# Interpolating attention biases along x on TensorE in every other block of keys, in the first image's heads

## The chip, the cores and the metric

The kernel runs on one core of a Trainium2 chip, as one launch. Its time is the device time of that core in microseconds; a kernel is run several times and the median is quoted. A core has five engines, each with its own queue of instructions that it works through in order: TensorE (PE in the profile; PEld is its loading of weights), VectorE (DVE), ScalarE (ACT), GpSimd (POOL) and SyncE (SP), which here only issues DMAs. Engines wait for each other through semaphores. Matmul results land in PSUM, which VectorE and ScalarE read; all other tiles lie in SBUF.

## The reference

The program takes four images of 32 x 32 positions with 384 channels through four layers. The change lies in the first layer, an attention with sampled keys (shortened):

```
q   = x @ w_q + b_q                                  # per image: 1024 positions, 6 heads of 64
pos = ref + tanh(offset network of q) * 16           # one sampling position per key and group
xs  = bilinear_sample(x, pos)
k, v = xs @ w_k + b_k, xs @ w_v + b_v
attn = einsum('bhmc,bnhc->bhmn', q, k) * 64**-0.5
disp = (ref of query m - pos of key n) * 0.5
bias = bilinear_sample(rpe table of the head, disp)  # one number per head, query and key
attn = softmax(attn + bias)
out  = einsum('bhmn,bnhc->bmhc', attn, v) @ w_out + b_out
```

For one key, all 1024 queries read the table at the same fractions in x and y, shifted by whole steps. So the biases of a key are a window of the table, interpolated along y with two weights and along x with two weights, all four belonging to that key alone. The layers behind it (a second attention, a normalisation by window sums and an attention over 3 x 3 neighbours) are not touched.

## The kernel before, in words

Images follow each other in two lanes. `Front` does the first layer, `Trunk` the other three. The first layer of image 0 stands alone at the start; those of images 1 to 3 are interleaved with the trunk. For image 0 the heads are done by `Front.heads0`, for the others by `Front.head0`, which the change leaves as it is. While `heads0` runs, only the first steps of image 1's front (`early0`: transposes, group norm) are put between its turns.

`heads0` walks over 96 blocks: 6 heads, 2 halves of the queries (512 each), 8 blocks of 128 keys. Keys lie on the 128 partitions, queries along the free axis, so a block is a tile of 128 x 512. `turn(t)` is one step of a software pipeline and issues work for several blocks, at fixed distances from t. Nearly every instruction is wrapped in `pin`, which keeps program order on its engine; the few that are not may be moved by the framework's scheduler. Tiles come from rings by tag, and a tile's first writer waits until the buffer's last reader is done.

Of block b, in the order in which its work comes:

- turn b - 10: POOL gathers the window of the bias table by an indirect DMA (`win`, L918, 6 buffers).
- turn b - 6: ACT starts the interpolation along y (`z`, L949, 4 buffers): the window's rows times one weight, 16 x 33 numbers a key.
- turn b - 5: DVE adds the rows below times the other weight (L930). ACT starts the interpolation along x (`lg`, L940, 20 buffers): columns 0 to 31 times one weight.
- turn b - 4: DVE adds columns 1 to 32 times the other weight (L935). `lg` now holds the biases.
- even turns: TensorE makes the products of keys and queries for blocks t + 2 and t + 3 (L960), into the two halves, two PSUM banks, of one of two `big` tiles. One 128 x 512 product of 32-bit numbers is two matmul instructions in the trace.
- turn b: DVE adds the product to `lg` (L980) and takes the running maximum over the blocks of the half (L985).
- at the end of a half's 8 blocks: TensorE transposes the maximum (L990), DVE reduces it (L971), POOL makes a diagonal (L975), TensorE multiplies it with ones (L1015) and ACT copies the result (`tb`, L994).
- turn b + 10: DVE subtracts `tb` (L999), ACT takes the exponential (L1000).
- turn b + 11: TensorE multiplies with the values and with ones (L1009), 64 columns of the array each.
- one turn after a half's last such product: ACT copies the result over the queries in `qpad` (L1024) and the denominator row into a dead `lg` tile (L1029), from which SP sends it to memory. Later `divide` brings the reciprocals back into two `lg` tiles and DVE multiplies.

Inside a turn the order on DVE is z, lg, (reduction,) add, maximum, subtraction; on ACT it is lg, the next block's z, (`tb`,) exponential; on POOL the gather, then the diagonal; on TensorE the products of the pair, (transposes,) the value products.

Of the kernel before, what the change touches and what calls it, by code (L numbers as in the profile page):

```python
# [21 lines left out]
ALU = mybir.AluOpType  # L22
# [393 lines left out]
class Front(Lane):  # L416
# [447 lines left out]
    def heads0(self, work):  # L864

        nc, v, pin = self.nc, self.nc.vector, self.tc.keep_in_program_order
        f, va = self.f, self.va
        HH, HN = HW // 2, N // 2  # L870
# [2 lines left out]
        n = len(blocks)  # L873

        AHEAD, SUB, OUT = 5, 10, 11
        win, z, lg, ps, half, dens, inv = {}, {}, {}, {}, {}, {}, {}

        def tile_of(shape, tag, bufs):
            return work.tile(shape, F32, tag=tag, name=self.nm(tag), bufs=bufs)
# [8 lines left out]
        def divide(step, k):  # L888
            heads = (2 * k, 2 * k + 1)
            by_row = lambda a: a.rearrange("o (p i) -> (o p) i", p=P)  # L890
            if step == 0:
                dens[k] = tile_of([P, 2, NJ], "dens", 2)
                for r, h in enumerate(heads):
                    nc.sync.dma_start(dens[k][:, r, :], by_row(self.den[h]))
            elif step == 1:
                pin(v.reciprocal(dens[k], dens[k]))
                for r, h in enumerate(heads):
                    nc.sync.dma_start(by_row(self.rden[h]), dens[k][:, r, :])
                for q in range(2):
                    inv[q] = tile_of([P, HN], "lg", 20)  # L900
                    for r, h in enumerate(heads):
                        nc.sync.dma_start(
                            inv[q][r * GC : (r + 1) * GC],
                            self.rden[h][0, q * HN : (q + 1) * HN].partition_broadcast(GC),
                        )
            else:
                for q in range(2):
                    out = queries(2 * k, q)
                    w = inv[q].rearrange("p (y x) -> p y x", x=HW)
                    pin(v.tensor_tensor(out, out, w, ALU.mult))  # L910

        def turn(t):
            i = t + AHEAD

            if i + 5 < n:
                h, q, j = blocks[i + 5]
                win[i + 5] = tile_of([P, (HH + 1) * WROW], "win", 6)
                nc.gpsimd.indirect_dma_start(  # L918
                    out=win[i + 5],
                    out_offset=None,  # L920
                    in_=self.strips[:, :],
                    in_offset=bass.IndirectOffsetOnAxis(
                        ap=self.widx[:, q, j * G + h : j * G + h + 1], axis=0
                    ),
                )
            at = lambda i: blocks[i][2] * G + blocks[i][0]
            sc = lambda i, axis, side: f[:, side, axis, at(i) : at(i) + 1]
            if 0 <= i < n:
                wv = win.pop(i).rearrange("p (r c) -> p r c", c=WROW)
                pin(v.scalar_tensor_tensor(  # L930
                    z[i], wv[:, 1 : HH + 1, 0 : HW + 1], sc(i, 1, 0), z[i], ALU.mult, ALU.add
                ))
            if 0 <= i - 1 < n:
                zi, lf = z.pop(i - 1), lg[i - 1].rearrange("p (y x) -> p y x", x=HW)
                pin(v.scalar_tensor_tensor(  # L935
                    lf, zi[:, :, 1 : HW + 1], sc(i - 1, 0, 0), lf, ALU.mult, ALU.add
                ))
            if 0 <= i < n:
                lg[i] = tile_of([P, HN], "lg", 20)
                pin(nc.scalar.activation(  # L940
                    lg[i].rearrange("p (y x) -> p y x", x=HW),
                    z[i][:, :, 0:HW],
                    AF.Copy,
                    scale=sc(i, 0, 1),
                ))
            if 0 <= i + 1 < n:
                wv = win[i + 1].rearrange("p (r c) -> p r c", c=WROW)
                z[i + 1] = tile_of([P, HH, HW + 1], "z", 4)
                pin(nc.scalar.activation(  # L949
                    z[i + 1], wv[:, 0:HH, 0 : HW + 1], AF.Copy, scale=sc(i + 1, 1, 1)  # L950
                ))

            if t >= -2 and (t + 2) % 16 == 0 and t + 18 < n and t + 2 >= 16:
                self.load_keys(blocks[t + 18][0])
            if t >= -2 and t % 2 == 0 and t + 2 < n:
                big = self.big()
                for u in range(2):
                    h, q, j = blocks[t + 2 + u]
                    ps[t + 2 + u] = big[:, u * 512 : (u + 1) * 512]
                    pin(nc.tensor.matmul(  # L960
                        ps[t + 2 + u],
                        self.kz[h % 2][:, j * P : (j + 1) * P],
                        queries(h, q),
                        start=True,
                        stop=True,
                    ))

            m = (t - 1) // NJ
            if t > 0 and t % NJ == 0 and t <= n:
                top = tile_of([P, NI], "top", 2)  # L970
                pin(v.tensor_reduce(  # L971
                    top, half[m, "t"].rearrange("p (i n) -> p i n", i=NI), AX.X, ALU.max
                ))
                diag = tile_of([P, NI, P], "diag", 1)
                pin(nc.gpsimd.tensor_tensor(  # L975
                    diag, bc(self.ident, 1, NI), bc(top, 2, P), ALU.mult
                ))
            if 0 <= t < n:
                m, j = divmod(t, NJ)
                pin(v.tensor_tensor(lg[t], ps.pop(t), lg[t], ALU.add))  # L980
                if j == 0:
                    half[m] = tile_of([P, HN], "rmax", 2)
                else:
                    first = lg[t - 1] if j == 1 else half[m]
                    pin(v.tensor_tensor(half[m], first, lg[t], ALU.max))  # L985
                if j == NJ - 1:
                    half[m, "t"] = self.bank()
                    for i in range(NI):
                        cols = slice(i * P, (i + 1) * P)
                        pin(nc.tensor.transpose(half[m, "t"][:, cols], half[m][:, cols], self.ident))  # L990
            if t > 1 and t % NJ == 1 and t <= n + 1:
                m = (t - 2) // NJ
                half[m, "b"] = tile_of([P, HN], "tb", 2)
                pin(nc.scalar.copy(half[m, "b"], half[m, "p"]))  # L994

            s = t - SUB
            if 0 <= s < n:
                tb = half[s // NJ, "b"]
                pin(v.tensor_tensor(lg[s], lg[s], tb, ALU.subtract))  # L999
                pin(nc.scalar.activation(lg[s], lg[s], AF.Exp))  # L1000

            o = t - OUT
            if 0 <= o < n:
                h, q, j = blocks[o]
                if j == 0:
                    half[o // NJ, "o"] = self.bank()
                po = half[o // NJ, "o"]
                for own, w in ((True, va[:, j, h * GC : (h + 1) * GC]), (False, self.ones[:, 0:GC])):
                    pin(nc.tensor.matmul(  # L1009
                        po[rows(h, own), :], w, lg[o], start=j == 0, stop=j == NJ - 1  # L1010
                    ))
            if t > 0 and t % NJ == 0 and t <= n:
                m = (t - 1) // NJ
                half[m, "p"] = self.bank()
                pin(nc.tensor.matmul(  # L1015
                    half[m, "p"], self.ones, diag.rearrange("p i n -> p (i n)"),
                    start=True, stop=True,
                ))

            o = t - OUT - 1  # L1020
            if 0 <= o < n and o % NJ == NJ - 1:
                h, q, j = blocks[o]
                po, own = half[o // NJ, "o"], rows(h, True)
                pin(nc.scalar.copy(  # L1024
                    queries(h, q)[own], po[own, :].rearrange("p (y x) -> p y x", y=HH)
                ))
                o0 = rows(h, False).start
                den = lg[o][o0 : o0 + 1, :]
                pin(nc.scalar.copy(den, po[o0 : o0 + 1, :]))  # L1029
                nc.sync.dma_start(self.den[h][:, q * HN : (q + 1) * HN], den)  # L1030

            o = t - OUT - 2
            for step, late in enumerate((0, 4, 9)):
                if o >= late and (o - late) % (4 * NJ) == 4 * NJ - 1:
                    divide(step, (o - late) // (4 * NJ))
# [831 lines left out]
```

## Time and profile before

| what | value |
|---|---|
| median of 3 runs | 4702.68 us (4702.3 to 4724.38) |
| the profiled execution: its own time | 4728.0 us |
| the profiled execution: span | 4726.2 us |
| busy over the span | PE 88%, DVE 68%, ACT 49%, POOL 20% |
| first product of keys and queries in `heads0` (L960) | 217.8 us |
| last product of keys and queries | 541.5 us |
| last value products (L1009) | 560.3 us |
| mean granted clock of TensorE, whole span | 0.927 |

Times inside the kernel are microseconds from the start of the profiled execution's span. In a line of the time line the columns are start, length, engine, source line, operation, tiles written and read, and in brackets the idle time before it with what ended that. In a table by stretch each engine has its busy time and, in brackets, its instructions; then come the granted TensorE clock as a share of full speed, the DMA engines' share and GB/s. A group's line gives the count, then busy time in us and mean length in ns, then idle time before. A shown length includes the filling and draining of the engine's pipeline, so the next instruction may start before the last has ended: the distance from start to start is the time that an instruction takes from its engine. A TensorE that is busy may still run at a lower clock.

### The profile page before, as it was taken

The page shows a single profiled execution, that of the slowest core. Times are in us where ns is not written, and L with a number is a line of the kernel's source. Part 1 is how long each engine was busy: PE and PEld are TensorE (multiplying, and loading weights), DVE is VectorE, ACT ScalarE, POOL GpSimd, SP SyncE. Part 2 cuts the span into 40 slices and gives each one's busy share as a digit, 9 for nine tenths or more (in the row PEclk, how much of TensorE's full clock was granted, in tenths as well). Part 3 has the DMA queues.
Part 4 walks back from the last instruction along what each step waited for, and adds up shares of the span by engine and source line. Part 5 has one row for each costly group of instructions (what it writes and reads, how often), then busy time and mean ns, then how long its engine had stood idle before and what let it go on. Part 6 is the DMA issues. An engine that isn't in the chain of part 4 may idle for free. (4 is left out here: it accounts for less than half of the span.)

```text
span 4726.2 us, 46786 instructions
## 1 busy us (share of the span) xinstructions
PE 4162.4 (88%) x15704; PEld 1784.0 (38%) x15704; DVE 3212.5 (68%) x6013; ACT 2295.6 (49%) x3631; POOL 944.9 (20%) x946
## 2 busy tenths in 40 slices
PE   5477788999999988899999989799999998999998
PEld 2222233333333353333333444243333335344444
DVE  3599756777878727587878763767787884565654
ACT  2166423566656313466666432346565651455532
POOL 0533204221212103321211110421121211000000
PEclk8688888999999988999999989899999998999998
DMA  6435224321212143321211124521121213311011
GB/s 122 132 112 151 66 93 127 95 64 54 70 37 68 54 142 117 116 69 51 79 53 55 58 78 116 157 85 55 37 79 51 74 37 110 110 27 30 19 40 40
DMA packets 231730, 369.98 MB, mean 78 GB/s; under 512 B 117508, under 2 KB 164705, under 8 KB 231489
## 3 DMA queue, kind: packets, MB, share of 16 engines
q1 hardware_dynamic: 170472, 200.51, 14.5%
q0 software_dynamic: 39936, 145.53, 10.5%
q10 hardware_dynamic: 21080, 20.96, 1.8%
q8 instruction: 124, 2.03, 0.2%
q14 instruction: 118, 0.96, 0.1%
HBM read 287.41 MB, written 79.78 MB: 78 GB/s over the span
## 5 line engine op out<-in xcount | busy, mean ns | idle before, releaser
L1479 PE MATMUL bank<-whole,sg 128*128 128x512 f32 (+3 forms) x2304 | 862.1, 509 | 8.7 <-POOL sg L1432 6.9
L1488 DVE SCALAR_TENSOR_TENSOR e<-bank,gam,e 128x512 f32<-128x512 f32 x768 | 562.2, 749 | 445.3 <-ACT gn L1487 159.0
L1331 ACT ACTIVATE big<-big,nmax 128x1024 f32<-128x1024 f32 x384 | 418.7, 1090 | 405.9 <-DVE nmax L1330 368.8
L1457 ACT ACTIVATE e<-big 128x1024 f32<-128x1024 f32 x384 | 379.8, 1019 | 410.1 <-PE big L1449 404.4
L1479 PEld LDWEIGHTS bank<-whole,sg 128*128 128x128 f32 x2304 | 407.2, 199 | 375.3 <-issue 284.4
L1330 DVE TENSOR_REDUCE nmax<-big 128x1 f32<-128x1024 f32 x384 | 454.8, 1219 | 75.1 <-PE big L1322 33.0
L797 POOL DMA_INDIRECT win<-strips,widx x288 | 307.7, 1069 | 686.9 <-DVE z L810 415.2
L1432 POOL TENSOR_SCALAR sg<-whole,gam 128x512 f32<-128x512 f32 x192 | 152.0, 794 | 1454.4 <-PE bank L1479 1005.2
L1449 PE MATMUL big<-qa,ka 64*128 64x512 f32 x1536 | 423.3, 623 | 8.8 <-ACT big L1331 8.6
L1322 PE MATMUL big<-k,q 32*128 32x512 f32 x1536 | 325.3, 681 | 68.1 <-ACT e L1457 41.8
L818 PE MATMUL bank<-qpad,kz 128*128 128x512 f32 x576 | 283.9, 622 | 12.5 <-DVE e L1488 12.5
L712 POOL DMA_INDIRECT gat<-pairs,sidx x192 | 204.3, 1064 | 436.7 <-DVE sidx L526 241.5
L853 PE MATMUL bank<-lg,va 128*64 128x512 f32 x576 | 264.9, 604 | 15.0 <-ACT lg L851 14.9
L853 PE MATMUL bank<-lg,ones 128*64 128x512 f32 x576 | 264.3, 603 | 0.0
L815 DVE SCALAR_TENSOR_TENSOR lg<-z,bias_f,lg 128x512 f32<-128x512 f32 x288 | 220.7, 775 | 41.0 <-ACT lg L814 38.7
L809 ACT ACTIVATE z<-win,bias_f 128x528 f32<-128x528 f32 x288 | 208.8, 739 | 68.6 <-DVE lg L815 29.7
L1449 PEld LDWEIGHTS big<-qa,ka 64*128 64x128 f32 x1536 | 137.7, 186 | 264.2 <-issue 153.4
L810 DVE SCALAR_TENSOR_TENSOR z<-win,bias_f,z 128x528 f32<-128x528 f32 x288 | 214.6, 763 | 26.8 <-ACT z L809 19.4
L850 DVE TENSOR_TENSOR lg<-lg,tb 128x512 f32<-128x512 f32 x288 | 187.4, 697 | 42.4 <-ACT tb L843 42.4
L1421 PE MATMUL bank<-e,vs 128*32 128x512 f32 x1536 | 206.7, 604 | 0.9 <-DVE vs L1415 0.9
L819 DVE TENSOR_TENSOR lg<-bank,lg 128x512 f32<-128x512 f32 x288 | 192.5, 685 | 21.7 <-PE bank L818 20.5
L814 ACT ACTIVATE lg<-z,bias_f 128x512 f32<-128x512 f32 x288 | 200.6, 720 | 13.6 <-PE bank L853 7.0
(302 smaller groups left out, 6646.2 us busy)
## 6 DMA issues: line engine op xcount, KB each, us to landing
pairs<-xn SPq DMA_DIRECT2D x64, 192.0 KB
q<-qd SPq DMA_DIRECT2D x48, 256.0 KB
w<-in_gmat SPq DMA_DIRECT2D x16, 576.0 KB
w<-in_w_off SPq DMA_DIRECT2D x12, 576.0 KB
w<-in_Wqkv SPq DMA_DIRECT2D x12, 576.0 KB
a<-in_x SPq DMA_DIRECT2D x16, 384.0 KB
x<-a ACTq DMA_DIRECT2D x4, 1536.0 KB
win<-strips,widx POOLq DMA_INDIRECT x384
```

Source lines behind the costliest of these rows:

```text
L797: nc.gpsimd.indirect_dma_start(out=win, out_offset=None, in_=self.strips[:, :], in_offset=bass.IndirectOffsetOnAxis(ap=self.widx[:, q, c : ...
L810: v.scalar_tensor_tensor(z, wv[:, 1 : HH + 1, 0 : HW + 1], sc(0, 1), z, ALU.mult, ALU.add)
L815: v.scalar_tensor_tensor(lg, z[:, :, 1 : HW + 1], sc(0, 0), lg, ALU.mult, ALU.add)
L818: nc.tensor.matmul(ps, kz[:, j * P : (j + 1) * P], both, start=True, stop=True)
L853: nc.tensor.matmul(po[out, :], w, lf, start=j == 0, stop=j == NJ - 1)
L1322: nc.tensor.matmul(ps[r][:, h * 512 : (h + 1) * 512], self.q4[rows, i * P : (i + 1) * P], self.k4[rows, 0:512], start=True, stop=True,)
L1330: v.tensor_reduce(nmax[:, r, i : i + 1], ps[r], AX.X, ALU.max, negate=True)
L1331: nc.scalar.activation(ps[r], ps[r], AF.Exp, bias=nmax[:, r, i : i + 1], accum_out=den[:, r, i : i + 1],)
L1449: nc.tensor.matmul(ps[:, r, :], ka[rows, j * P : (j + 1) * P], qa[rows, cols], start=True, stop=True,)
L1457: nc.scalar.activation(e, ps, AF.Exp)
L1479: nc.tensor.matmul(ps[:, (mid - i0) * P :], sg[:, r, m, :], sim[:, h, r, m, (mid - i0) * P :], start=m == 0, stop=m == 1,)
L1488: v.scalar_tensor_tensor(e[:, r, :], ps, self.gam[:, 1:2], e[:, r, :], ALU.add, ALU.mult, accum_out=tot[:, r, h : h + 1],)
```

## The change

In every odd block of keys the interpolation along x and the addition to the logits move from ACT and DVE to TensorE. POOL writes two diagonal matrices a block (`dg`), with the two x weights of the 128 keys on the diagonals. TensorE multiplies columns 0 to 31 of `z` with one and columns 1 to 32 with the other, and accumulates both and the product of keys and queries in one PSUM bank. ACT copies the finished logits out of PSUM (`lp`, a ring of its own with 7 buffers), and DVE takes the running maximum straight from PSUM. Even blocks stay as they were. The rings change: `lg` from 20 to 10 buffers, `z` from 4 to 6, `dg` has 3. The denominator row is copied into the half's `tb` tile instead of an `lg` tile.

```diff
-                    inv[q] = tile_of([P, HN], "lg", 20)
+                    inv[q] = tile_of([P, HN], "lg", 10)
...
-            if 0 <= i - 1 < n:
+            if 0 <= i - 1 < n and i % 2:
                 zi, lf = z.pop(i - 1), lg[i - 1].rearrange("p (y x) -> p y x", x=HW)
...
-            if 0 <= i < n:
-                lg[i] = tile_of([P, HN], "lg", 20)
+            if 0 <= i < n and i % 2:
+                dg[i] = tile_of([P, 2, P], "dg", 3)
+                pin(nc.gpsimd.tensor_tensor(
+                    dg[i],
+                    bc(self.ident, 1, 2),
+                    bc(f[:, :, 0, at(i) : at(i) + 1].rearrange("p s o -> p (s o)"), 2, P),
+                    ALU.mult,
+                ))
+            elif 0 <= i < n:
+                lg[i] = tile_of([P, HN], "lg", 10)
                 pin(nc.scalar.activation(
...
-                z[i + 1] = tile_of([P, HH, HW + 1], "z", 4)
+                z[i + 1] = tile_of([P, HH, HW + 1], "z", 6)
...
-                    pin(nc.tensor.matmul(
-                        ps[t + 2 + u],
-                        self.kz[h % 2][:, j * P : (j + 1) * P],
-                        queries(h, q),
-                        start=True,
-                        stop=True,
-                    ))
+                    terms = [(self.kz[h % 2][:, j * P : (j + 1) * P], queries(h, q))]
+                    if u:
+                        zi, di = z.pop(t + 3), dg.pop(t + 3)
+                        terms[:0] = [
+                            (di[:, 1, :], zi[:, :, 0:HW]),
+                            (di[:, 0, :], zi[:, :, 1 : HW + 1]),
+                        ]
+                    for k, (w, a) in enumerate(terms):
+                        pin(nc.tensor.matmul(
+                            ps[t + 2 + u], w, a, start=k == 0, stop=k == len(terms) - 1
+                        ))
...
-                pin(v.tensor_tensor(lg[t], ps.pop(t), lg[t], ALU.add))
+                if t % 2:
+                    lg[t] = tile_of([P, HN], "lp", 7)
+                    pin(nc.scalar.copy(lg[t], ps[t]))
+                else:
+                    pin(v.tensor_tensor(lg[t], ps[t], lg[t], ALU.add))
...
-                    pin(v.tensor_tensor(half[m], first, lg[t], ALU.max))
+                    pin(v.tensor_tensor(half[m], first, ps[t] if t % 2 else lg[t], ALU.max))
...
-                den = lg[o][o0 : o0 + 1, :]
+                den = half[o // NJ, "b"][o0 : o0 + 1, :]
```

In the changed kernel the lines are: z on ACT L958 and on DVE L931, the diagonals L941, the lg scaling L949 and interpolation L936 (even blocks), the products L977, the copy L995, the add L997, the maximum L1002, the subtraction L1016, the exponential L1017, the value products L1026. On ACT an odd turn issues, in the built order, the lg scaling of block t + 5, z of block t + 6, the copy of block t, the exponential of block t - 10; an even turn issues z of block t + 6 and the exponential. An even turn t writes the diagonals of block t + 5, after its gather on POOL.

More of the change, by code (lines that the diff above doesn't have):

```diff
@@ L875, in heads0 @@
         AHEAD, SUB, OUT = 5, 10, 11
-        win, z, lg, ps, half, dens, inv = {}, {}, {}, {}, {}, {}, {}
+        win, z, dg, lg, ps, half, dens, inv = {}, {}, {}, {}, {}, {}, {}, {}
         def tile_of(shape, tag, bufs):
```

## The prediction

> **What bounds the kernel now.** The change touches one stage, the heads of image 0, so I first asked where it lies and which engine sets its pace. The source view of the logits product gives its place: first at 217.5 us, last at 541.5, with the last value products at 560.3. Then busy time by stretch. The columns after the stretch and its length are PE, PEld, DVE, ACT, POOL, the granted TensorE clock and DMA:
>
> ```profile
> 217.00:226.00 9.00, 4.39 (x11) 1.71 (x10) 5.74 (x9) 4.24 (x7) 3.65 (x3) 0.91 0.75 247
> 256.00:300.00 44.00, 30.98 (x92) 9.44 (x92) 43.58 (x68) 29.05 (x46) 17.81 (x15) 0.88 0.34 99
> 300.00:364.00 64.00, 49.74 (x156) 19.19 (x154) 58.63 (x98) 39.25 (x64) 21.21 (x19) 0.82 0.45 141
> 364.00:545.00 181.00, 143.67 (x395) 43.95 (x392) 178.55 (x273) 114.98 (x184) 61.54 (x52) 0.86 0.40 111
> ```
>
> DVE is busy 43.58 of 44 us and 178.55 of 181: it is the bound. TensorE looks 79% busy, but at a granted clock of 0.82 to 0.88 and with overlapping ends. ACT has a third of its time free. Next one block of keys on the time line, DVE and ACT together:
>
> ```profile
> 427.48 0.68 DVE L999 TENSOR_TENSOR lg<-lg,tb 128x512 f32<-128x512 f32 x1
> 428.08 0.76 DVE L930 SCALAR_TENSOR_TENSOR z<-win,bias_f,z 128x528 f32<-128x528 f32 x1
> ...
> 428.20 0.63 ACT L1000 ACTIVATE lg<-lg 128x512 f32<-128x512 f32 x1 [0.47 <-DVE lg L999]
> ...
> 428.76 0.75 DVE L935 SCALAR_TENSOR_TENSOR lg<-z,bias_f,lg 128x512 f32<-128x512 f32 x1
> 428.88 0.73 ACT L940 ACTIVATE lg<-z,bias_f 128x512 f32<-128x512 f32 x1
> ...
> 429.42 0.68 DVE L980 TENSOR_TENSOR lg<-big,lg 128x512 f32<-128x512 f32 x1
> 429.51 0.72 ACT L949 ACTIVATE z<-win,bias_f 128x528 f32<-128x528 f32 x1
> ...
> 430.14 0.69 DVE L985 TENSOR_TENSOR rmax<-rmax,lg 128x512 f32<-128x512 f32 x1
> 430.75 0.68 DVE L999 TENSOR_TENSOR lg<-lg,tb 128x512 f32<-128x512 f32 x1
> 431.35 0.76 DVE L930 SCALAR_TENSOR_TENSOR z<-win,bias_f,z 128x528 f32<-128x528 f32 x1
> ```
>
> A turn is 428.08 to 431.35, 3.27 us. Its parts, start to start: z 0.68, lg 0.66, add 0.72, max 0.61, subtraction 0.60. ACT in the same turn does the exponential, then (once DVE's z has ended, at 428.84) the lg scaling at 428.88, then the next z at 429.51. Half a head is 8 turns, a reduction (0.60) and a DVE stall by POOL's diagonal: 8 x 3.27 would be 26.2, and starts eight blocks apart (419.7 to 446.4) give 26.7. The groups of the stretch 226 to 545 supply the other prices:
>
> ```profile
> L999 DVE TENSOR_TENSOR lg<-lg,tb 128x512 f32<-128x512 f32 x85 | 64.5, 759 | 0.0
> ...
> L975 POOL TENSOR_TENSOR diag<-ident,top 128x512 f32<-128x512 f32 x11 | 11.5, 1047 | 14.4 <-DVE top L971 14.2
> ...
> L994 ACT COPY tb<-bank 128x512 f32<-128x512 f32 x11 | 6.5, 587 | 17.1 <-PE bank L1015 17.1
> ```
>
> And TensorE at full clock:
>
> ```profile
> 426.28 1.99 PE L960 MATMUL big<-qpad,kz 128*128 128x512 f32 x4
> 428.19 0.64 PE L1009 MATMUL bank<-lg,va 128*64 128x512 f32 x1
> 428.20 0.64 PE L1009 MATMUL bank<-lg,ones 128*64 128x512 f32 x1
> ```
>
> Four matmul instructions (two products, each two instructions) hold the path 1.91 us until the value products: 0.43 each and 0.19 to change over. Value and denominator products run side by side.
>
> **The change, part by part.**
>
> *DVE work removed and added.* Turn t interpolates block t+4 and adds block t; for odd t both are odd blocks, so odd turns lose the lg interpolation (L935) and the add (L980), and even turns keep all five operations, 3.27 us. An odd turn keeps z, max and subtraction: 0.68 + 0.60 (the max now reads PSUM; the add's row, 0.68 long with the next operation 0.60 on where nothing depends on it) + 0.60 = 1.88. Alone that would be a gain of 1.39 us a pair, 66 us in 48 pairs.
>
> *The wait added.* In the built program's list of waits the odd max (new L1002) waits for ACT's copy of the same PSUM bank (L995), not only for TensorE: both engines read that bank. The copy stands on ACT behind the lg scaling (L949) and the next z (L958) of the same turn, and that scaling waits for DVE's z of this turn. So DVE waits for a chain that its own first operation starts. From the odd turn's start: z ends at 0.76; lg scaling starts at 0.80 (428.08 to 428.88); next z at 1.43 (429.51); copy 0.64 later, at 2.07 (an ACT operation that follows z starts that much later, z being 0.72 long and starts overlapping); copy 0.59 long (L994's row, 587 ns, the same shape from PSUM), end 2.66; max at 2.70; subtraction at 3.30; next turn at 3.90. The odd turn grows from 3.27 to 3.90: +0.63. Queued behind the waiting max on DVE are the subtraction and the next turn's z; for those wait the exponential, the next lg scaling and the value products, and TensorE's next pair waits for the max itself, since it frees the bank. 45 odd turns (t = 1 to 89) have the full chain: 45 x 0.63 = **+28.4**.
>
> The Trainium skill's page "PSUM — Partial Sum Buffer", section "PSUM bank collisions raise a hardware error", says that two engines reading one bank at once is an error and that nothing in the chip arbitrates. No run here shows a collision. By that rule the wait cannot simply be dropped, but it asks only for the copy's own 0.59 us, which with the copy first on ACT would leave the odd turn near 2.5 us, a gain; the row's queue order makes it 3.90.
>
> *The last three odd turns* (91, 93, 95) have no z or lg left. Today they take 0.72 + 0.61 + 0.60 = 1.93. After: the exponential of the even turn ends its slot at 0.65, the copy ends at 1.24, max at 1.28, then 1.21: 2.49. 3 x 0.56 = **+1.7**.
>
> *The start.* From 218.5 to 226.4 a turn takes 2.19 today, because each z on ACT stands behind an lg scaling. Even turns lose that scaling and take DVE's 1.34: two pairs x 0.85 = **-1.7**.
>
> *Fewer lg buffers.* 20 become 10 for even blocks, and two are held by the division's factors. In the list of waits six lg scalings (blocks 54, 56, 58, 86, 88, 90) wait for the value product of the block 16 earlier, whose exponential follows the last subtraction: 0.12 + 0.63 + 0.05, product 1.08 (0.48 + 0.60), 0.05: start at 1.93 instead of 0.80. Here the chain is longer by 1.13: 6 x 1.13 = **+6.8**. Bounds: 0 if ACT had that time to spare (the chain above leaves none), 6 x 2.2 if TensorE comes to it one product late.
>
> *Two more products a pair on TensorE.* 4 more instructions, 4 x 0.43 = 1.7 us: a pair takes 1.91 + 1.72 + 1.87 (four value steps, 436.19 to 438.06) = 5.5 us of 7.17. Cover: DVE's wait. The pair starts after the odd max and is wanted by an add 9.1 us later (subtraction 0.6, turns of 3.27 and 3.90, z and lg 1.34), so even at half clock (8 starts 0.85 apart, as at 457.9 us, 7.0 us) it is in time. I take **0**; from below nothing, since no TensorE time goes; from above 12 late transposes at about 0.5, 6 us, or more if the clock stays low (a rival).
>
> *Diagonals on POOL.* 48 of 128x256; half of L975's 1047 ns is 0.52 us each. That L999 averages 759 against 684 comes from this: beside POOL's diagonal it takes 1.34. A diagonal follows a window gather, which starts after DVE's z: from 2.2 to 2.8 of the odd turn, while DVE waits or reads PSUM. I take **0**; from above 48 x 0.33 (0.65 lost per 1.05) = 16 us. The Trainium skill's page "SBUF — State Buffer", section "Who interferes with whom", calls the shared port an exclusive lock for whole instructions, against a VectorE operation with two SBUF inputs. An estimate by that rule, if each met one, is 48 x 0.52 = 25 us.
>
> *The front of image 1, interleaved.* Its ACT copies (16 of 0.47) can lengthen the chain, its DVE statistics (6 of 0.6) can fill the wait: -3 to +6, taken as **0**. The denominator row now leaves from the tb tile; its next writer comes six turns later, about 20 us: 0. Window gathers on POOL and SP's key loads keep their places relative to the turns: 0.
>
> **Sum:** 28.4 + 1.7 - 1.7 + 6.8 = +35.2 us, on the profiled execution's own 4728.0 (span 4726.2): 4763. That execution stands 25.3 above the median of the runs, 4702.7; the stage's queues are the same in both, so I add it to the median: **4738 us**.
>
> **The rivals.**
> 1. *DVE is not held*: the copy is always done before the max. Then TensorE bounds: half a head takes 4 x 5.5 + 0.53 (transposes, 546.59 to 547.12) + 1.05 (the product with ones, 549.54 to 550.59) = 23.6 against 26.7, 12 x 3.1 = 37 us less, 4666, at full clock. For it: ACT is a third free and DVE loses 66 us of work. Against it: the copy's place behind a scaling that the same turn's z releases. It decides if the copy starts before 0.1 us of the odd turn. Chance 4%.
> 2. *The chain is there but partly paid*: statistics fill it, the six lg waits vanish, the copy is shorter than 0.59. 28 less a few: 4705 to 4726, which cannot be told from no change (0.5%, 23.5 us, is about what a measurement tells here). 12%.
> 3. *TensorE is late too*: the clock is granted at half where gaps fall between pairs. At half clock a pair takes about 10.5 us (twice 0.43 x 12 and change-overs) against 7.17; if a fifth of 48 pairs lose 3.3 each, 32 us on top, 4770. For it: 0.82 to 0.88 granted today. Against: TensorE will be busier, and from 650 us, at 49.4 of 50 us busy, the clock was 1.00. It decides once it is late by more than the 2 us between 7.0 and 9.1 in several pairs running. 9%.
>
> **How the numbers follow.** The forecast has 75%, by itself 4726 to 4765. Slower by over 0.5%: 75 + 9 = 84%; within: 12%; faster: 4%. The range, 4716 to 4770, takes in the upper part of rival 2 and the lower of rival 3, the lock's 16 and the interleaved front's bounds.
>
> **What would show it.** In the profile after: DVE near 75% busy from 256 us on, not 98%; odd max waits of about 2 us put down to ACT's copy, some 90 us in 45 turns; odd turns of 3.9 and even ones of 3.3; 29.9 us per half head; the stage's end near 595 us; six longer waits of ACT for the value products; TensorE's matmuls of L977 at full clock more often than today. If DVE stays full and the stage ends before 545, the wait is not where I put it; if DVE waits on TensorE instead, rival 3 holds.

## The result and the profile after

The changed kernel takes 4768.5 us (median of 4 runs, 4761.1 to 4772.4) against 4708.9 us for the kernel before in 4 runs. The ratio is 1.0123 with a 95% interval of 1.0100 to 1.0146: it is slower, by 1.0 to 1.5%. The profiled execution has a span of 4759.3 us and a time of 4761.1.

The rise lies in the stage that was changed. From the start of the first product of keys and queries to the end of the last value product, `heads0` took 343.1 us before (217.8 to 560.9) and takes 393.7 us after (216.2 to 610.0): 50.6 us more. What follows it took 4165 us before and 4149 after, single profiles of kernels whose runs differ by that much (22 us among those of before). The stage of the kernel before rests on one profile. Below I compare stages wherever a profile is there, and ratios for the whole.

The head of the page of the changed kernel:

```profile
span 4759.3 us, 47142 instructions
...
PE 4217.1 (89%) x15896; PEld 1812.6 (38%) x15896; DVE 3155.4 (66%) x5917; ACT 2287.5 (48%) x3631; POOL 959.5 (20%) x994
```

Over the span hardly anything has moved: VectorE from 68% to 66%, TensorE and ScalarE by a point. The stretches of the stage show it (after the stretch and its length: PE, PEld, DVE, ACT, POOL, granted clock, DMA share, GB/s):

```profile
256.00:300.00 44.00, 38.23 (x105) 13.44 (x104) 32.06 (x49) 24.72 (x41) 16.42 (x19) 0.92 0.31 92
300.00:364.00 64.00, 55.92 (x188) 22.09 (x187) 51.36 (x83) 38.15 (x63) 24.11 (x27) 0.97 0.45 146
364.00:480.00 116.00, 93.32 (x263) 32.94 (x264) 74.82 (x112) 59.13 (x100) 38.68 (x45) 0.91 0.44 119
480.00:545.00 65.00, 53.36 (x149) 18.13 (x146) 44.71 (x68) 34.72 (x57) 23.43 (x27) 0.96 0.29 86
```

VectorE, which was busy 98 to 99% of most of this time, is busy 73, 80, 64 and 69% in the four rows (32.06 of 44, and so on). No other engine has taken its place: TensorE is busier than before, at 87, 87, 80 and 82%, but not full, and ScalarE is at 51% in the third row. When no engine is full, a chain of waits sets the pace. Its place is on the time line of an odd turn of the changed kernel, VectorE and ScalarE:

```profile
459.97 0.76 DVE L931 SCALAR_TENSOR_TENSOR z<-win,bias_f,z 128x528 f32<-128x528 f32 x1
...
460.76 0.72 ACT L949 ACTIVATE lg<-z,bias_f 128x512 f32<-128x512 f32 x1
...
461.39 0.73 ACT L958 ACTIVATE z<-win,bias_f 128x528 f32<-128x528 f32 x1
...
462.14 0.59 ACT L995 COPY lp<-big 128x512 f32<-128x512 f32 x1
...
462.76 0.69 DVE L1002 TENSOR_TENSOR rmax<-rmax,big 128x512 f32<-128x512 f32 x1 [2.03 <-ACT lp L995]
...
463.37 0.68 DVE L1016 TENSOR_TENSOR lp<-lp,tb 128x512 f32<-128x512 f32 x1
...
463.97 0.76 DVE L931 SCALAR_TENSOR_TENSOR z<-win,bias_f,z 128x528 f32<-128x528 f32 x1
```

VectorE's z releases ScalarE's scaling 0.79 us later, the next z follows at 1.42, the copy at 2.17, the maximum at 2.79, and the turn ends at 4.00. This one is a little long; the next odd turn, 467.24 to 471.16, takes 3.92, and where the wait is the usual 1.89 us a turn takes 3.87. VectorE does three operations in it and stands still for half of it. Over the stage (226 to 600 us; the columns are the total in us, the times and the longest):

```profile
DVE rmax L1002 <- ACT lp L995: 106.8, 44, 8.0
```

38 of the 44 waits are short, 70.7 us together, 1.86 on the mean. The other six are 6.40, 4.72, 7.95 and 6.64, 4.72, 5.69 us, 36.1 together, in two groups of three. They make two half heads long. The last six distances between adds eight blocks apart are 27.4, 28.0, 26.7, 26.7, 27.0, 28.0 us before the change and 29.5, 44.3, 29.5, 29.4, 29.4, 42.6 us after it. The groups of ScalarE in the same stretch name what the six wait for:

```profile
L949 ACT ACTIVATE lg<-z,bias_f 128x512 f32<-128x512 f32 x45 | 32.5, 722 | 44.7 <-PE bank L1026 25.0 <-DVE z L931 17.9
```

The scaling writes a new `lg` tile, and six times (25.0 us) it waits for a value product: the last reader of the buffer that it is to have.

### The profile page after: what moved, and what is told of

It is laid out like the page before. It is cut to its first block, busy times and chain, and to the rows that moved or that the text cites. A ratio compares the mean times of both kernels' runs of the same rounds, so it can differ in the third digit from the quotient of the medians.

```text
span 4759.3 us, 47142 instructions
## 1 busy us (share of the span) xinstructions
PE 4217.1 (89%) x15896; PEld 1812.6 (38%) x15896; DVE 3155.4 (66%) x5917; ACT 2287.5 (48%) x3631; POOL 959.5 (20%) x994
## 5 line engine op out<-in xcount | busy, mean ns | idle before, releaser
L1347 DVE TENSOR_REDUCE nmax<-big 128x1 f32<-128x1024 f32 x384 | 454.6, 1219 | 61.8 <-PE big L1339 30.5
L819 DVE TENSOR_TENSOR lg<-bank,lg 128x512 f32<-128x512 f32 x288 | 192.4, 685 | 23.4 <-PE bank L818 22.3
```

Source lines behind the costliest of these rows:

```text
L1347: v.tensor_reduce(nmax[:, r, i : i + 1], ps[r], AX.X, ALU.max, negate=True)
```

## The experiments

All runs stand against the kernel before on the same chip. Chips differ: the kernel before took 4710.7 us beside the first four runs, 4680.7 beside the next three and 4713.5 beside the last three, so ratios and stages are compared, not times. The stage is taken from each run's profile as above; before's is 343.1 us.

| run | ratio to before (95%) | stage, us | stage against before, us |
|---|---|---|---|
| a0_after, the changed kernel again | 1.0115 (1.0087 to 1.0142) | 394.4 | +51.3 |
| e1_max_first | 0.9978 (0.9960 to 0.9997) | 326.9 | -16.2 |
| e2_lg12 | 1.0076 (1.0052 to 1.0100) | 371.5 | +28.4 |
| e3_both | 0.9933 (0.9909 to 0.9958) | 313.7 | -29.4 |
| e4_noprod | 1.0075 (1.0056 to 1.0093) | 381.6 | +38.5 |
| e5_copy_early | 0.9973 (0.9960 to 0.9987) | 335.1 | -8.0 |
| e7_three | 0.9939 (0.9920 to 0.9958) | 325.3 | -17.8 |
| e3_again | 0.9940 (0.9924 to 0.9956) | 313.6 | -29.5 |
| e8_dg_on_act | 0.9948 (0.9931 to 0.9965) | 311.5 | -31.6 |
| e9_early_lg12 | 0.9971 (0.9956 to 0.9986) | 321.7 | -21.4 |

The stage repeats within 1 us (393.7 and 394.4; 313.7 and 313.6), which is finer than the ratios.

### The changed kernel again: a0_after

> The changed kernel again, for the others to be compared with on the same chip. Both theories: 4761 to 4772 us, 1.01 to 1.015 of before.

4760.3 us against 4710.7. It is the row that the others are measured against.

### The maximum ahead of the copy: e1_max_first

```diff
-                if t % 2:
-                    lg[t] = tile_of([P, HN], "lp", 7)
-                    pin(nc.scalar.copy(lg[t], ps[t]))
-                else:
+                if t % 2 == 0:
                     pin(v.tensor_tensor(lg[t], ps[t], lg[t], ALU.add))
...
                     pin(v.tensor_tensor(half[m], first, ps[t] if t % 2 else lg[t], ALU.max))
+                if t % 2:
+                    lg[t] = tile_of([P, HN], "lp", 7)
+                    pin(nc.scalar.copy(lg[t], ps[t]))
```

> The changed kernel with one thing turned round: in odd turns DVE takes the maximum out of PSUM first, and ACT copies the bank after it, so the maximum no longer waits for the copy. Theory A (DVE held in each odd turn by the copy that stands behind a chain on ACT): the waits of 1.9 us put down to the copy are gone, odd turns fall from 3.87 to about 1.9 us, the pair from 7.14 to what TensorE allows, 5.5 to 6.0; half heads of 24 to 25 us in place of 29.5. The six waits for lg buffers stay, 3 to 6 us each. In all 45 to 65 us less than the changed kernel: 4705 to 4725. Theory B (TensorE's two more products a pair are what the stage got slower by): the pair stays near 7 us, the wait only moves to TensorE, 0 to 10 us less.

4695.9 us, some 9 us better than the expected 4705 to 4725. The stage falls by 67.5 us and the ratio by 1.4%, without an instruction less. Of the six waits of ScalarE's scaling for a value product four are left, 13.6 us in all. An odd turn on the time line of this run, VectorE's lines and the copy:

```profile
456.76 0.76 DVE L931 SCALAR_TENSOR_TENSOR z<-win,bias_f,z 128x528 f32<-128x528 f32 x1
...
457.44 0.67 DVE L999 TENSOR_TENSOR rmax<-lg,big 128x512 f32<-128x512 f32 x1
...
458.04 0.68 DVE L1016 TENSOR_TENSOR lp<-lp,tb 128x512 f32<-128x512 f32 x1
...
458.87 0.56 ACT L1002 COPY lp<-big 128x512 f32<-128x512 f32 x1
...
459.00 1.00 DVE L931 SCALAR_TENSOR_TENSOR z<-win,bias_f,z 128x528 f32<-128x528 f32 x1 [0.28 <-ACT z L958]
```

The maximum stands right behind z, the copy takes place beside other work, and the turn is 2.24 us. The two readers of the bank still take turns; ScalarE, which has time, now goes second. So the wait was the cost, not the work.

### More lg buffers: e2_lg12

```diff
-                    inv[q] = tile_of([P, HN], "lg", 10)
+                    inv[q] = tile_of([P, HN], "lg", 12)
...
-                lg[i] = tile_of([P, HN], "lg", 10)
+                lg[i] = tile_of([P, HN], "lg", 12)
...
-                z[i + 1] = tile_of([P, HH, HW + 1], "z", 6)
+                z[i + 1] = tile_of([P, HH, HW + 1], "z", 5)
```

> The changed kernel with two more lg buffers (12 for 10), room for which comes from one z buffer (5 for 6). Theory A: the six long waits of ACT's lg scaling for value products 16 blocks back are gone (they then ask for products 20 back), the maximum's six waits of 4.7 to 8 us fall to the usual 1.9, 25 us less than the changed kernel: 4743. Theory B: those waits are TensorE being late, they only move elsewhere, 0 to 5 us less.

The room for the two buffers comes from the `z` ring, which has one buffer less. 4739.1 us; the stage falls by 22.9 us, from 394.4 to 371.5. The line of waits and the group of the scaling in this run:

```profile
DVE rmax L1002 <- ACT lp L995: 82.6, 44, 2.5
```

```profile
L949 ACT ACTIVATE lg<-z,bias_f 128x512 f32<-128x512 f32 x45 | 32.4, 720 | 19.9 <-DVE z L931 17.9 <-PE big L977 0.2
```

The 25.0 us of waiting for value products are gone, no wait for the copy is over 2.5 us, and the two long half heads go from 42.8 and 42.6 to 31.0 and 31.5. The half heads between them stay at 29.3 to 29.4: the usual wait is untouched.

### Both: e3_both and e3_again

The edits of e1_max_first and e2_lg12 together.

> Both edits together: the maximum first, and 12 lg buffers. Theory A: DVE is held by neither, TensorE becomes the bound with 5.5 us a pair and 23.6 to 25 us a half head; 65 to 90 us less than the changed kernel, 4680 to 4705, at or below before. Theory B: 0 to 15 us less, 4755 to 4770.

> e3_both once more, so that the next two kernels stand beside it on the same chip: 0.9933 of the time before, between 0.991 and 0.996.

4671.3 and 4683.3 us: faster than the kernel before by 0.4 to 0.9% in the first run and by 0.4 to 0.8% in the second. The third stretch of e3_both:

```profile
364.00:480.00 116.00, 116.00 (x349) 40.41 (x350) 108.84 (x158) 78.25 (x133) 59.53 (x63) 1.00 0.52 142
```

TensorE is busy through all 116 us at full clock, VectorE for 94% of them. Here TensorE's added products should cost time; no run takes them out of this version. In the changed kernel this state is not reached in any of the four stretches.

### TensorE without the added products: e4_noprod

```diff
                     terms = [(self.kz[h % 2][:, j * P : (j + 1) * P], queries(h, q))]
                     if u:
                         zi, di = z.pop(t + 3), dg.pop(t + 3)
-                        terms[:0] = [
-                            (di[:, 1, :], zi[:, :, 0:HW]),
-                            (di[:, 0, :], zi[:, :, 1 : HW + 1]),
-                        ]
```

> The changed kernel without its two products of z with the diagonals on TensorE: the bias of every second block in the first image's heads is left out of the scores, all else (diagonals on GpSimd, copy, waits, buffers) stays. Theory A (the time comes from VectorE's wait for ScalarE's copy in the odd turns and from the lg buffers, not from TensorE's work): the usual odd turn keeps its 3.87 us and its wait of 1.9 us; the six long waits get shorter by the 1.7 us of the two products that no longer stand ahead of the value product, at most by the 3.4 us that they take at half clock. That is 10 to 20 us off the changed kernel's 4760: 4740 to 4750 us. Theory B (TensorE's added products carry the rise): 4700 to 4715 us, as before the change.

4717.8 us, on the faster chip; by ratio 0.4% under the changed kernel, 19 us, and by stage 12.8 us. The wait for the copy and the scaling's group in this run (their lines are L998, L991 and L949):

```profile
DVE rmax L998 <- ACT lp L991: 96.3, 44, 4.9
```

```profile
L949 ACT ACTIVATE lg<-z,bias_f 128x512 f32<-128x512 f32 x45 | 32.4, 720 | 33.1 <-DVE z L931 17.6 <-PE bank L1022 13.6
```

The usual wait is 1.89 us as before (one of the 38 short ones went from 1.29 to 2.74) and the undisturbed half heads are 29.4 and 29.5 as before: 96 products less, and next to nothing moves there. What moves are the six long waits, now 4.93, 3.06, 4.72 and 4.92, 3.07, 3.69: 24.4 us in place of 36.1 (34.6 in the repeat, whose first wait is 5.04 in place of 6.40). Four of them are shorter than in the first profile by 1.5 to 1.7 us, which is about the products' four instructions at 0.43 us, the other two by 2.0 and 3.2. Theory A holds, and it gets a detail: TensorE's added work costs something where ScalarE waits for TensorE, in those six turns.

### The copy first on ScalarE: e5_copy_early

```diff
         def turn(t):
             i = t + AHEAD

+            if 0 <= t < n and t % 2:
+                lg[t] = tile_of([P, HN], "lp", 7)
+                pin(nc.scalar.copy(lg[t], ps[t]))
...
-                if t % 2:
-                    lg[t] = tile_of([P, HN], "lp", 7)
-                    pin(nc.scalar.copy(lg[t], ps[t]))
-                else:
+                if t % 2 == 0:
                     pin(v.tensor_tensor(lg[t], ps[t], lg[t], ALU.add))
```

> The changed kernel with ScalarE's copy of an odd block put at the head of the odd turn, ahead of the scaling into lg and of the next z; VectorE's maximum still comes after the copy. Theory A1 (VectorE waits because of the copy's place in ScalarE's queue, behind a scaling that itself waits for VectorE's z of the same turn): the copy runs while VectorE is still at its z, the 45 waits of 1.9 us go down to 0 to 0.6 us, and the kernel loses 45 x 1.3 to 45 x 1.9 = 58 to 85 us against 4760, less what ScalarE's scaling and z lose by coming 0.57 us later: 4690 to 4715 us, with the six long waits for lg buffers moved off the maximum or left in part. Theory A2 (it is the sharing of one PSUM bank by the two readers itself, wherever the copy stands): the waits stay and the time stays within 10 us of 4760 us.

4668.0 us on the faster chip; by ratio 1.4% under the changed kernel, some 67 us, and by stage 59.3 us. An odd turn on the time line of this run:

```profile
454.97 0.76 DVE L934 SCALAR_TENSOR_TENSOR z<-win,bias_f,z 128x528 f32<-128x528 f32 x1
455.09 0.63 ACT L1017 ACTIVATE lg<-lg 128x512 f32<-128x512 f32 x1 [2.37 <-DVE lg L1016]
...
455.62 0.57 ACT L918 COPY lp<-big 128x512 f32<-128x512 f32 x1
...
456.09 0.72 ACT L952 ACTIVATE lg<-z,bias_f 128x512 f32<-128x512 f32 x1
456.22 0.69 DVE L1002 TENSOR_TENSOR rmax<-rmax,big 128x512 f32<-128x512 f32 x1 [0.49 <-ACT lp L918]
456.71 0.73 ACT L961 ACTIVATE z<-win,bias_f 128x528 f32<-128x528 f32 x1
456.83 0.69 DVE L1016 TENSOR_TENSOR lp<-lp,tb 128x512 f32<-128x512 f32 x1
456.97 1.02 POOL L944 TENSOR_TENSOR dg<-ident,bias_f 128x256 f32<-128x256 f32 x1
...
457.48 1.08 DVE L934 SCALAR_TENSOR_TENSOR z<-win,bias_f,z 128x528 f32<-128x528 f32 x1
```

The maximum still comes after the copy, and the turn is 2.51 us in place of 3.87 to 4.00. The copy starts behind the exponential, the wait left is 0.49 us, and the scaling that used to stand ahead of it comes 0.47 us behind the copy's start. Over the stage the waits put down to the copy (total in us, times, longest) are:

```profile
DVE rmax L1002 <- ACT lp L918: 21.3, 36, 1.5
```

So of the usual wait of 1.89 us, 1.4 is the copy's place in ScalarE's queue; the 0.5 that is left is the end of a copy of 0.57 us that itself stands behind the exponential. Theory A1 holds. The prediction weighed a rule of the Trainium skill, page "PSUM — Partial Sum Buffer", section "PSUM bank collisions raise a hardware error", that software must keep two engines off one bank at a time. No run here let them collide; e1_max_first and e5_copy_early show that keeping the rule costs VectorE nothing in a turn with the maximum first and 0.5 us with the copy at the head of ScalarE's turn.

### The same with more lg buffers: e9_early_lg12

The edits of e5_copy_early and e2_lg12 together.

> e5_copy_early with lg 12 in place of 10 and z 5 in place of 6. In e5_copy_early two half heads took 32.9 and 31.3 us where the others took 24.9; if the lg buffers are what those two wait for, they go to 25 or 26 us and the time is 12 to 15 us under e5_copy_early's 0.9973 of before: 0.994 to 0.995. Against e3_again it stays behind by the half heads' 24.9 against 23.4 us, eleven times 1.5 = 16 us, because its maximum still waits about 0.5 us for the copy in every odd turn. If the long half heads in e5_copy_early have another cause, it stays at 0.997.

The ratio, 0.9971, misses 0.994 to 0.995 and can't be told from e5_copy_early's. The stage meets the expectation: 321.7 against 335.1, 13.4 us less, the two long half heads down from 32.9 and 31.3 to 26.2, and ScalarE's waits for value products, 13.9 us in e5_copy_early, gone. Its stage is 8.1 us longer than e3_again's, where 16 were expected. The runs don't settle where the whole kernel lost the stage's gain. In its profile nothing is lost: that execution took 4689.1 us, the third fastest of twelve, and what follows the stage took 4148 us there against 4152 in the profile of e3_again.

### Three blocks of eight: e7_three

The edit is shown against e3_both; the ring sizes (13 `lg`, 6 `lp`) and the operand of the maximum change with it.

```diff
+        te = lambda b: b % 2 and b % 8 != 7
...
-            if 0 <= i - 1 < n and i % 2:
+            if 0 <= i - 1 < n and not te(i - 1):
...
-            if 0 <= i < n and i % 2:
+            if 0 <= i < n and te(i):
...
-                    if u:
+                    if te(t + 2 + u):
...
-                if t % 2 == 0:
+                if not te(t):
                     pin(v.tensor_tensor(lg[t], ps[t], lg[t], ALU.add))
...
-                if t % 2:
+                if te(t):
```

> As e3_both (maximum ahead of the copy, more lg buffers), with only the first three odd blocks of each eight on the diagonals' path, so that the last block of each half head is made as before the change; buffers: lg 13, lp 6, z 5. Theory A says that in e3_both TensorE is the bound in the middle of the stage, with about 24 us for a half head: one pair less of products of 1.7 us gives TensorE about 22 us for each half head, and VectorE, with the scaling and the addition back for one block, about 22.5 us. Ten half heads by 1.5 us: 4650 to 4665 us against e3_both's 4671. If VectorE's chain is still the bound there, it gets slower instead: 4675 to 4690 us.

4656.2 us looks like the expected time, but only because this chip was the faster one: the ratio, 0.9939, is e3_both's, and the stage, 325.3 us, is 11.6 longer. The third stretch and the diagonals' group there:

```profile
364.00:480.00 116.00, 105.20 (x321) 35.62 (x318) 111.22 (x159) 79.10 (x132) 57.38 (x55) 1.00 0.51 140
```

```profile
L942 POOL TENSOR_TENSOR dg<-ident,bias_f 128x256 f32<-128x256 f32 x14 | 12.3, 876 | 0.3
```

VectorE is busy 96% and is the bound again, at 24.8 to 24.9 us for a half head, not the 22.5 expected. I had left out that VectorE and GpSimd lengthen each other. The diagonals here take 876 ns where they took 624 in the same stretch of e3_both, and the subtraction of an `lp` tile 872 ns against 682; that this makes up the whole difference is not worked out. By the stage, four blocks in eight are the better mix; the ratios do not tell the two apart.

### The diagonals off GpSimd: e8_dg_on_act

```diff
-                pin(nc.gpsimd.tensor_tensor(
-                    dg[i],
-                    bc(self.ident, 1, 2),
-                    bc(f[:, :, 0, at(i) : at(i) + 1].rearrange("p s o -> p (s o)"), 2, P),
-                    ALU.mult,
-                ))
+                for side in range(2):
+                    pin(nc.scalar.activation(
+                        dg[i][:, side, :], self.ident, AF.Copy, scale=sc(i, 0, side)
+                    ))
```

> e3_both with the two diagonals of an odd block made by ScalarE (two scaled copies of the identity) in place of one operation on GpSimd. In e3_both 41 of the 48 GpSimd operations met VectorE's z and lengthened it to about 1.02 us, 13.4 us over the stage in all, while TensorE was busy in all of the 116 us from 364 to 480. Theory TensorE bounds that version: VectorE's 13.4 us hide, the time stays within 5 us of e3_again. Theory the GpSimd operations cost what they lengthen: 10 to 14 us less than e3_again. If ScalarE's two more operations (some 0.3 us each, 48 x 0.6 = 29 us, on an engine that is busy for 60 of 116 us) delay its z or its scaling, the time rises instead, by up to 29 us.

4686.9 us against e3_again's 4683.3, and 311.5 us of stage against 313.6. VectorE's z over 256 to 530 us, first in e3_both, then here:

```profile
L931 DVE SCALAR_TENSOR_TENSOR z<-win,bias_f,z 128x528 f32<-128x528 f32 x79 | 68.5, 867 | 9.0 <-ACT z L958 6.8 <-issue 1.9
```

```profile
L931 DVE SCALAR_TENSOR_TENSOR z<-win,bias_f,z 128x528 f32<-128x528 f32 x78 | 59.5, 762 | 17.3 <-ACT z L956 14.7 <-issue 2.3
```

VectorE gets back 105 ns a z, 8 us, and spends it waiting for ScalarE's z, 14.7 us in place of 6.8. (Over the stage the 41 z in e3_both are 10.7 us longer by their own lengths, not the 13.4 expected.) The 8 us hide. That TensorE bounds that version fits, since it is busy 116.00 of 116 us from 364 to 480 in both; but ScalarE has two more operations in each odd block here, and this run does not rule out that they took the gain.

## Why the prediction was right, and where it was off

The prediction was 4738 us, in a range of 4716 to 4770, and slower with 0.84. The measured 4768.5 is slower, at the range's upper end and 3.5 us above the likeliest case's own range. Point by point:

- **What bounds, and which wait comes.** As forecast: VectorE is no longer full, and the place of its work is taken by the odd maximum's wait for ScalarE's copy. The chain came out nearly step by step: scaling 0.80 us after the turn's start forecast and 0.79 found in the turn shown, z 1.43 and 1.42, copy 2.07 and 2.17, maximum 2.70 and 2.79, end 3.90 and 4.00, with 3.87 in the usual turn. VectorE's work in an odd turn did get shorter; only the wait is longer than the work saved. e1_max_first and e5_copy_early, which change the order alone, show that this wait is what made the change slower.
- **45 odd turns, +28.4; last three, +1.7; start, -1.7.** Together +28.4, and e2_lg12, in which only these and the terms put at nothing are left, measures 371.5 - 343.1 = +28.4 us of stage. The agreement to the tenth is luck: the last three waits are 1.17, 1.31 and 1.17 us (forecast: 1.28), but the start gained only 0.1 from the first product to the first add (8.59 to 8.45 us). And the two half heads in which image 1's statistics run on VectorE grew from 30.8 and 33.6 to 31.0 and 34.3 us in e2_lg12, not by 4 x 0.63 = 2.5 each; that interleaved work, put at nothing, seems to have hidden part of the wait, which was not tested.
- **Fewer lg buffers, +6.8, bounds 0 and 13.2: the mis-sized term.** The six waits were found where they were forecast, but the stage lost 22.9 us by them (a0_after less e2_lg12). The step that failed is the one that lets the value product start 0.05 us after the exponential and take 1.08 us. In the wait shown here it ends 4.5 us after the exponential instead. On the time line of the changed kernel:

```profile
396.99 1.08 PE L1007 MATMUL bank<-ident,rmax 128*128 128x128 f32 x4 [2.55 <-DVE rmax L1002]
...
398.92 1.06 PE L1026 MATMUL bank<-lg,va 128*64 128x512 f32 x1
...
399.91 1.13 PE L977 MATMUL big<-qpad,kz 128*128 128x512 f32 x2
400.88 1.88 PE L977 MATMUL big<-z,dg 128*128 128x512 f32 x4
...
401.52 0.63 ACT L1017 ACTIVATE lg<-lg 128x512 f32<-128x512 f32 x1 [3.40 <-DVE lg L1016]
...
402.60 1.02 PE L977 MATMUL big<-qpad,kz 128*128 128x512 f32 x2
...
403.55 0.64 PE L1026 MATMUL bank<-lp,va 128*64 128x512 f32 x1
...
404.56 1.12 PE L1032 MATMUL bank<-diag,ones 128*128 128x512 f32 x2
...
406.09 0.59 PE L1026 MATMUL bank<-lg,va 128*64 128x512 f32 x1
...
406.79 0.72 ACT L949 ACTIVATE lg<-z,bias_f 128x512 f32<-128x512 f32 x1 [4.64 <-PE bank L1026]
...
408.64 0.69 DVE L1002 TENSOR_TENSOR rmax<-lg,big 128x512 f32<-128x512 f32 x1 [6.40 <-ACT lp L995]
...
409.38 1.31 PE L977 MATMUL big<-qpad,kz 128*128 128x512 f32 x2 [2.69 <-DVE rmax L1002]
```

  The exponential of the block that is waited for ends at 402.15. Its value product stands on TensorE behind the rest of the pair, the other block's value products and the product with ones, and ends at 406.7. Only then does ScalarE go on; the maximum ends the chain at 408.64, and TensorE, which needs that maximum for the next pair's bank, stands still for 2.69 us. I had priced TensorE as if it were free, with "one product late" as the upper bound, while the same text has the value products behind a pair of 3.6 us in the queue. The queue had been written down for TensorE's load and not for this wait.
- **Two more products on TensorE, 0.** Right in the 38 usual turns (e4_noprod: one wait of them moved), wrong in the six long ones, where 10 to 12 of the 23 to 25 us above the usual wait go with the products (the repeat and the first profile against e4_noprod): they lengthen the queue just described. With the wait gone they should bound the stage (e3_both).
- **Rival 3, TensorE late at half clock.** It was part of the truth in the six turns. In the wait shown the granted clock was 0.51 from 397 to 400 us, and the work ahead of the pair took 2.92 us, from 396.99 to 399.91. In the repeat, a0_after, the same work took 1.57 us at a granted clock of 1.00, and the wait is shorter by as much:

```profile
399.62 0.63 PE L1007 MATMUL bank<-ident,rmax 128*128 128x128 f32 x4 [1.55 <-DVE rmax L1002]
...
401.19 1.13 PE L977 MATMUL big<-qpad,kz 128*128 128x512 f32 x2
...
404.82 0.64 PE L1026 MATMUL bank<-lp,va 128*64 128x512 f32 x1
...
409.92 0.69 DVE L1002 TENSOR_TENSOR rmax<-lg,big 128x512 f32<-128x512 f32 x1 [5.04 <-ACT lp L995]
```

  A pair takes 3.63 us here (401.19 to 404.82). In the wait of 7.95 us of the changed kernel, behind a standstill of 4.43 us, it takes 6.69, with a granted clock of 0.55 from 421 to 428 us:

```profile
421.08 2.08 PE L977 MATMUL big<-qpad,kz 128*128 128x512 f32 x2 [4.43 <-ACT qpad L1041]
...
427.77 0.64 PE L1026 MATMUL bank<-lp,va 128*64 128x512 f32 x1
```

  Added up over the six waits, what the same work took beyond these 1.57 and 3.63 us is 1.35, 1.70, 3.06, 1.58, 1.69 and 1.50, together about 11 us. That is my estimate of the slow clock's part in the long waits of the first profile; it overlaps with the part of the added products, which took longer there too. The slow stretches follow standstills of TensorE of 2.55 to 4.43 us, where a0_after's full-speed one follows 1.55; what sets the clock was not tested. The prediction had weighed the half clock for the add that waits for the pair, where there was time, and not for the value products that stand behind the pair.
- **Rival 1, VectorE not held.** It did not happen, but e3_both makes it happen, and its sum stands: 23.6 us a half head were forecast, 23.4 to 25.4 are found in the last six, with TensorE busy throughout from 364 to 480 us.
- **Diagonals on GpSimd, 0.** Right here: only 6 of VectorE's z met one, 1.6 us in all, because VectorE waits at that moment. Without the wait the cover goes: in e3_both 41 z met one and took about 1.02 us. The Trainium skill's page "SBUF — State Buffer", section "Who interferes with whom", whose lock gave an estimate of 25 us, agrees that a VectorE operation with two SBUF inputs is held up. The amount is smaller than a lock over the whole overlap would make it: 0.44 us of overlap cost 0.25.
- **The other marks.** The stage ended at 610.0, not 595, by the lg term. VectorE is 64 to 80% busy, around the 75 forecast. TensorE's clock in these stretches is 0.91 to 0.97, up from 0.82 to 0.88, as forecast.

Of the 30.5 us between forecast and median, 16 are the lg term (22.9 less 6.8), and 6 are the kernel before, at 4708.9 in these runs and 4702.7 in those that the sum was put on. The remaining 8 are inside the interval of the ratio, 47 to 69 us of rise.

## What to carry to other kernels

When work is moved off the bound engine, look at what the new work makes that engine wait for: in this program two engines that read one PSUM bank take turns in program order, and the one with time to spare should go second (64 us here, for three moved lines). Price a wait on a recycled buffer by the whole queue ahead of its last reader, at the clock that the trace shows there, and not by that reader's own length. When a stage shows no engine full, count its waits before cutting more work: with two waits mended, the same change made the kernel 0.6 to 0.7% faster in place of 1.2% slower.

## What the runs showed of the hardware that was not expected

- GpSimd's 128 x 256 diagonals take 0.62 us alone (half of the 128 x 512 one's 1047 ns, 0.52, had been assumed). Beside VectorE, what grows depends on what they meet and on which came first. In e3_both VectorE's z typically starts 0.19 us behind the diagonal: 40 diagonals stay at 0.62 and the z takes about 1.02 in place of 0.76. In the turn of e5_copy_early shown above the diagonal starts 0.14 us behind the subtraction: the subtraction keeps its 0.69, the diagonal takes 1.02 and the z behind it 1.08. In e7_three both can grow, to 0.88 for the subtraction and 1.02 for the diagonal. How busy VectorE is does not set the price by itself: it is at 94% in e3_both, with diagonals of 0.62, and at 96% in e7_three, with 0.88 on the mean (both from 364 to 480 us).
- TensorE's granted clock differs between versions by enough to change a stage's sums: 0.82 to 0.88 before, 0.91 to 0.97 in the changed kernel, 1.00 in the middle stretch of e3_both. A matmul instruction of the pairs took 744 ns on the mean before, 649 after and 610 in e3_both. Here the added products cost less than their count times the old duration.
- ScalarE writes one scaled 128 x 128 copy of the identity in 0.39 us, two for a block, against 0.62 us for both on GpSimd, and VectorE's z goes back to 762 ns from 867 (e8_dg_on_act).
